# A 2-D Fourier layer whose residual rides through its own backward transform, with both w transforms as four 64x64 tiles

## The chip, the cores and the metric

One NeuronCore of one Trainium2 chip runs the whole program in one launch. The metric is device microseconds (us) of an execution; lower is better. A core has a tensor engine (PE, whose weight loads are listed apart as PEld), a vector engine (DVE), a scalar engine (ACT), GpSimd (POOL) and a sync engine (SP) that here issues all the transfers. Each engine runs its own instructions in order and waits on semaphores for the others.

## The reference, cut to what matters

`x` has two images of 48 x 48 tokens with 768 channels, float32.

```python
# --- layer 0: group norm, then attention over all 2304 tokens with relative positions
x = x + _L0_conv_ref(_gn(x), qkv_w, qkv_b, proj_w, proj_b, rel_pos_h, rel_pos_w)
# --- layer 1: group norm, then a block-diagonal complex MLP between two Fourier transforms
x = x + _L1_conv_ref(_gn(x), w1, b1, w2, b2)

def _L1_conv_ref(x, w1, b1, w2, b2):           # 8 blocks of 96 channels
    xf = jnp.fft.rfft2(x, axes=(1, 2), norm='ortho')          # 48 x 25 frequencies
    o1r = gelu(xr @ w1[0] - xi @ w1[1] + b1[0]);  o1i = gelu(xi @ w1[0] + xr @ w1[1] + b1[1])
    o2r = o1r @ w2[0] - o1i @ w2[1] + b2[0];      o2i = o1i @ w2[0] + o1r @ w2[1] + b2[1]
    xc = softshrink(o2r, 0.01) + 1j * softshrink(o2i, 0.01)
    return jnp.fft.irfft2(xc, s=(48, 48), axes=(1, 2), norm='ortho')
```

The second `x +` is the residual of this case: the layer's input has to be added to what the backward transform gives.

## The kernel before

All arithmetic is float32. Both images' attention comes first, in one pipelined loop (`attention`). Then, for each image in turn, come `project_out` and `Spectral.run`. Between the images, the second image's projection loads are prepared while the first image's spectral part ends.

`project_out` makes the output of layer 0 and starts the Fourier transform over w. There are 18 tiles of 128 tokens (t) in two halves of 384 channels (hf). `pr.product(t, hf)` is six matmuls into a PSUM bank called `acc`. `rows(i)` loads four 96-token rows of the input into a tile `x2[i]` (96 partitions hold two image rows) and POOL adds the projection bias, one instruction for each of the four. DVE adds the product onto `x2` (L941), in pieces given by `shifts(t)`, because 128-token tiles and 96-token rows do not line up. When two rows' worth is ready, `over_w(g)` multiplies it by the transform matrix `fw` (L920, banks `ps_y`), ACT copies the result to `y1` (L927), and SP writes it to a scratch tensor `y_d` in device memory. The first three products' six banks are already filled at the end of attention (`late.fill`).

`Spectral` works on four groups s of 192 channels, each of two blocks n of 96. `load` brings group s back from `y_d` (tiles `y2`, queue entries `y<-y_d`). `over_h(n)` is the transform over h (banks `ps_z`), `mean` and `norm` the group norm, `first(n)` and `second(n)` the two layers of the MLP (banks `ps_1`, `ps_2`). After the second block of a group, `back_h(j)` transforms back over h (banks `ps_u`) and writes a scratch tensor `u_d`. `back_w(s, more)` first, if s is at least 0, multiplies the loaded `u2` tiles by `iw` (L1213, banks `ps_x`). DVE adds the result onto `x2` (L1221), which has held the residual all along, and SP sends that part of `x2` to the output. In the same loop it loads the next group's `u2` from `u_d`. `back_w` is called with s = -1 at block 2, s = 0 at block 4, s = 1 at block 6, s = 2 at the end, and then s = 3 with `more=False`.

Seven PSUM banks are shared by everything except attention's `ps_o`. Order on an engine is chosen by the framework's scheduler from dependences; what goes through `InOrder` keeps its program order (and is recorded as L68, the helper's line, so such work is told apart by its tiles). SP's queue is in order too: an entry that waits holds up all entries behind it.

Of the kernel before, what the change touches and what calls it, by code (L numbers as in the profile page):

```python
# [42 lines left out]
YP = 112  # L43
# [232 lines left out]
def attention(tc, k, xs, a, oTs, inv_ds, late, span, ps_b, ps_o):  # L276
# [12 lines left out]
    with ExitStack() as ctx:  # L289
# [263 lines left out]
        def finish(un):  # L553

            pr, g, x = un["pr"], un["g"], un["x"]
            if x == 0:
                outs[pr, g] = outp.tile([P, 8, 3, 16], F32, tag="res", name="res")
                if g % 3 == 0:
                    dens[pr, g // 3] = outp.tile([P, 3, 2, 3], F32, tag="dens", name="dens")
            res = outs[pr, g]  # L560
            act.copy(res[:, :, x, :], un["o"][:, :P].rearrange("p (y d) -> p y d", d=16))
            dve.tensor_reduce(
                dens[pr, g // 3][:, x, :, g % 3], un["parts"], AX.X, ALU.add
            )
            if x == 2:
                sync.dma_start(
                    out=oTs[pr // NP][pr % NP * P : (pr % NP + 1) * P, g * UQ : (g + 1) * UQ],
                    in_=res.rearrange("p y x d -> p (y x d)"),
                )

        def inverses(pr, half):
# [12 lines left out]
            def send():  # L584
                dst = inv_ds[pr // NP][pr % NP, half].rearrange("h g (y x d) -> x (h g) y d", x=3, d=16)
                for x in range(3):
                    sync.dma_start(
                        out=dst[x],
                        in_=turned[6 * x : 6 * x + 6, :].rearrange("p (y d) -> p y d", d=16),
                    )  # L590
# [155 lines left out]
def shifts(t):  # L746


    size = {0: P, 32: 32, 64: 64, 96: 32}
    p = 0  # L750
    while p < P:
        hp, q = divmod(t * P + p, 2 * HW)
        n = min(P - p, 2 * HW - q, size[p], size[q])
        yield p, hp, q, n
        p += n


class Projection:
# [27 lines left out]
    def cut(self, whole, i):  # L786

        return whole[:, self.head + i * NCC * UQ :][:, : NCC * UQ]
# [10 lines left out]
    def w(self):  # L799
        return self.fixed()[:, : NCC * C].rearrange("p (cc f) -> p cc f", f=C)  # L800

    @property
    def pb(self):
        return self.fixed()[:, NCC * C : self.head]
# [82 lines left out]
def project_out(tc, k, x_b, pr, pools, y_d, x2, constants):  # L887
# [7 lines left out]
    ps_b, work = pools  # L895
    bank = lambda name: ps_b.tile([P, 512], F32, tag="b", name=name)
    R = 2 * HW
    x_v = x_b.rearrange("(t p) c -> p t c", p=R)

    def rows(i):  # L900

        part = x2[i]
        pr.sync.dma_start(out=part, in_=x_v[:, i * XP : (i + 1) * XP, :])
        for j in range(XP):
            pr.pool.tensor_tensor(part[:, j, :], part[:, j, :], pr.pb[:R], ALU.add)
# [4 lines left out]
    row = lambda hp: x2[hp // XP][:, hp % XP, :]  # L910

    def over_w(g, steps=range(C // SC)):

        y1 = work.tile([YP, 2, C], F32, tag="y1", name="y1")
        part = x2[2 * g // XP]
        t0 = 2 * g % XP
        for s in steps:
            ch = slice(s * SC, (s + 1) * SC)
            ps = bank("ps_y")
            nc.tensor.matmul(  # L920
                ps[:YP, : 2 * SC],
                lhsT=k.fw,
                rhs=part[:, t0 : t0 + 2, ch],
                start=True,
                stop=True,
            )
            nc.scalar.copy(y1[:, :, ch], ps[:YP, : 2 * SC].rearrange("p (t c) -> p t c", c=SC))  # L927
        ch = slice(steps[0] * SC, (steps[-1] + 1) * SC)
        pr.sync.dma_start(out=y_d[:, 2 * g : 2 * g + 2, ch], in_=y1[:, :, ch])

    turned = 0
    for t in range(NT):
        if t % 3 == 0 and 0 < t < NT - 3:
            pr.tokens(t // 3 + 1)
            rows(t // 3 + 1)
        for hf in range(2):
            cols = slice(hf * UQ, (hf + 1) * UQ)
            acc = pr.product(t, hf)
            for p, hp, q, n in shifts(t):
                dst = row(hp)[q : q + n, cols]  # L940
                nc.vector.tensor_tensor(dst, acc[p : p + n, :UQ], dst, ALU.add)  # L941
            if t == NT - 1:
                half = C // SC // 2
                for g in range(turned, HW // 4):
                    over_w(g, range(hf * half, (hf + 1) * half))
        while t < NT - 1 and (turned + 1) * 2 * R <= (t - 1) * P:
            over_w(turned)
            turned += 1
# [3 lines left out]
class Spectral:  # L952
# [12 lines left out]
    def __init__(self, tc, k, a, pools, x2, y_d, out_b, prepare):  # L965
        self.tc, self.nc, self.k, self.a, self.prepare = tc, tc.nc, k, a, prepare
        self.sync = InOrder(tc, tc.nc.sync)
        self.span, self.ps_b, self.small, self.wp, self.yp, self.up, self.dp, zp = pools
        self.x2, self.y_d = x2, y_d
        self.out_v = out_b.rearrange("(t p) c -> p t c", p=2 * HW)  # L970
# [21 lines left out]
        self.y2, self.u2, self.w, self.power = {}, {}, {}, {}  # L992
# [57 lines left out]
    def norm(self, n):  # L1050
# [24 lines left out]
        for f0 in range(0, NF, 400):  # L1075
            fs = slice(f0, f0 + 400)
            nc.gpsimd.tensor_tensor(self.both[n % 2][:, fs], zf[:, 0, fs], zf[:, 1, fs], ALU.add)

    def load(self, s, pieces):

        src = self.y_d[: 4 * KW, :, s * SC : (s + 1) * SC].rearrange(
# [7 lines left out]
    def over_h(self, n):  # L1089
# [7 lines left out]
        for j in range(KW // WP):  # L1097
# [13 lines left out]
            if n == 1 and j == 1:  # L1111
                self.mean(0)
            if n == 1 and j == 3:
# [30 lines left out]
    def second(self, n, ahead):  # L1144
# [9 lines left out]
        for j in range(KW // WP):  # L1154
# [22 lines left out]
            nc.gpsimd.tensor_tensor(val, val, clip, ALU.subtract)  # L1177
# [25 lines left out]

    def back_w(self, s, more):


        nc, k = self.nc, self.k
        ch = slice(s * SC, (s + 1) * SC)
        u_d = self.u_d.rearrange("w (q t) c -> (w q) t c", q=4)
        for i, part in enumerate(self.x2):  # L1210
            for t in range(0, XP, 2) if s >= 0 else ():
                ps = self.bank("ps_x")
                nc.tensor.matmul(  # L1213
                    ps[: 2 * HW, : 2 * SC],
                    lhsT=k.iw,
                    rhs=self.u2[s, i][:, t : t + 2, :],
                    start=True,
                    stop=True,
                )
                dst = part[:, t : t + 2, ch]  # L1220
                nc.vector.tensor_tensor(  # L1221
                    dst, ps[: 2 * HW, : 2 * SC].rearrange("p (t c) -> p t c", c=SC), dst, ALU.add
                )
            if more:
                u2 = self.up.tile([4 * KW, XP, SC], F32, tag="u2", name="u2")
                self.sync.dma_start(out=u2, in_=u_d[:, i * XP : (i + 1) * XP, :])
                self.u2[s + 1, i] = u2
            if s >= 0:
                self.sync.dma_start(
                    out=self.out_v[:, i * XP : (i + 1) * XP, ch], in_=part[:, :, ch]  # L1230
                )

    def run(self):
# [12 lines left out]
        for n in range(NBK + 1):  # L1246
# [6 lines left out]
            if n:  # L1253
                self.second(n - 1, ahead)
# [15 lines left out]
def block_kernel(tc, a, out):  # L1270
    nc = tc.nc
    B = a["x"].shape[0]
    with ExitStack() as ctx:
# [21 lines left out]
        for b in range(B):  # L1295
            oTs.append(dram.tile([C, S], F32, tag=f"oT{b}", name=f"oT{b}"))
            y_ds.append(dram.tile([YP, HW // 2, C], F32, tag=f"y_d{b}", name=f"y_d{b}"))
# [26 lines left out]
        attention(tc, k, a["x"], a, oTs, inv_ds, late, span, ps_b, ps_o)  # L1324
        for b in range(B):
            with ExitStack() as ctx2:
# [3 lines left out]
                x2 = [  # L1330
                    pool(f"x2_{i}", 1).tile([2 * HW, XP, C], F32, tag="x2", name=f"x2_{i}")
                    for i in range(HW // 2 // XP)
                ]
# [113 lines left out]
```

## Time and profile before

| what | value |
|---|---|
| median of 3 runs | 3661.01 us (3660.04 to 3662.53) |
| the profiled execution | 3660.19 us, span 3658.4 us |
| granted TensorE clock, mean | 0.987 |
| attention | to about 2838 us of the span |
| image 0: `project_out`, then `Spectral` | 2838 to 2988, then to about 3236 us |
| image 1: `project_out`, then `Spectral` | 3236 to 3409, then to 3658 us |

In the profile PE's and the other engines' busy times are of instructions that work, not of those that wait. A float32 matmul is recorded as two MATMUL rows. "idle before" is the time an engine sat idle just ahead of a group, and the arrow names what released it. Queue entries are listed under SPq with the time that their issue took.

### The profile page before, as it was taken

Reading aid. Unit: us, or ns where it says so; the run is one execution under the profiler, and the core shown is the slowest. Engines: PE = TensorE matmul, PEld = TensorE weight load, DVE = VectorE, ACT = ScalarE, POOL = GpSimd, SP = SyncE. Lnnn points to the kernel's source line nnn. Section 1 sums busy time; section 2 is a strip of 40 time slices with the busy share of each in tenths; the row PEclk is TensorE's granted clock in tenths of the full one; section 3 lists DMA queues with packets and bytes.
Section 4 is the critical chain, followed back from the end, with each engine's and each line's share of the span. In section 5 each row is a group of like instructions: output and inputs, shape, how many; then the busy total and the mean of one; then the engine's idle time right before and its main releaser. Section 6 shows DMA issues by size and latency. Waiting matters only on the chain.

```text
span 3658.4 us, 92606 instructions
## 1 busy us (share of the span) xinstructions
PE 3548.6 (97%) x36032; PEld 2477.2 (68%) x36032; DVE 2902.1 (79%) x6771; ACT 2557.2 (70%) x3769; POOL 2047.2 (56%) x662
## 2 busy tenths in 40 slices
PE   7999999999999999999999999999988999999898
PEld 5677676767767666677676767767666557655675
DVE  4798989989989996799898989899996437743576
ACT  3788888888888888688888888888885124301342
POOL 2567666757575763567666666666673524343232
PEclk9999999999999999999999999999999989999999
DMA  3687778777777885677777777777888743585434
GB/s 105 142 181 171 180 171 179 172 179 171 181 169 175 214 200 122 140 178 174 176 176 171 177 173 175 176 176 172 188 190 190 200 127 85 169 213 147 109 110 140
DMA packets 496484, 607.61 MB, mean 166 GB/s; under 512 B 179117, under 2 KB 311597, under 8 KB 496046
## 3 DMA queue, kind: packets, MB, share of 16 engines
q1 hardware_dynamic: 496046, 601.68, 69.3%
q8 instruction: 286, 4.69, 0.6%
q14 instruction: 152, 1.25, 0.1%
HBM read 131.60 MB, written 87.67 MB: 60 GB/s over the span
## 4 chain that ended last, share of the span: by engine, by line
PE 84%; DVE 5%; ACT 3%; DMA 3%; issue 2%; POOL 1%; SPq 1%; POOLq 0%; DVEq 0%; ACTq 0%
PE ps_o L68 22%; PE ps_s L68 21%; PE ps_proj L68 15%; PE ps_v L68 8%; PE acc L68 7%; DVE s L68 2%; PE ps_u L1195 2%; PE ps L1160 2%; PE ps_y L920 2%; PE ps_r L68 2%; SPq L68 1%; PE ps_x L1213 1%; DMA pT<-s 1%; ACT spectrum L1035 1%; POOL s L68 1%
## 5 line engine op out<-in xcount | busy, mean ns | idle before, releaser
L68 POOL TENSOR_TENSOR s<-rhw 128x2304 f32<-128x2304 f32 x432 | 1740.8, 4062 | 1025.3 <-DMA pT<-s 546.8
L68 DVE CUSTOM_DVE_ANT_0 s<-ps_s,s 128x512 f32<-128x512 f32 (+1 forms) x2160 | 1222.2, 633 | 299.7 <-issue 196.1
L68 ACT ACTIVATE s<-s,nm 128x1152 f32<-128x1152 f32 x864 | 1074.7, 1245 | 335.3 <-DVE nm L68 333.1
L68 DVE STREAM_TRANSPOSE s<-s 128x1152 f32<-128x1152 f32 x864 | 1112.0, 1344 | 6.8 <-ACT s L68 6.8
L68 ACT COPY pT<-s 32x1152 f32<-32x1152 f32 x864 | 993.6, 1150 | 25.9 <-PE ps_o L68 7.5
L68 PE MATMUL ps_o<-pT,v 128*64 128x128 f32 x15552 | 906.5, 276 | 41.7 <-ACT res L68 18.9
L68 PEld LDWEIGHTS ps_o<-pT,v 128*64 128x64 f32 x15552 | 875.4, 139 | 84.0 <-issue 43.6
L68 PE MATMUL ps_s<-kT,qT 64*128 64x512 f32 (+1 forms) x4320 | 899.8, 554 | 4.9 <-DVE mx L68 1.7
L68 PEld LDWEIGHTS ps_s<-kT,qT 64*128 64x128 f32 x4320 | 432.3, 186 | 418.1 <-issue 347.0
L68 PE MATMUL ps_proj<-xnT,w 128*64 128x384 f32 (+1 forms) x4032 | 591.3, 446 | 4.9 <-ACT xnT L68 3.7
L68 PEld LDWEIGHTS ps_proj<-xnT,w 128*64 128x64 f32 x4032 | 281.0, 137 | 278.8 <-issue 212.1
L941 DVE TENSOR_TENSOR x<-acc,x 32x384 f32<-32x384 f32 (+2 forms) x216 | 119.2, 553 | 227.8 <-PE acc L68 163.8
L68 PE MATMUL ps_v<-w,xnT 128*64 128x128 f32 x5184 | 297.3, 274 | 0.0
L68 PEld LDWEIGHTS ps_v<-w,xnT 128*64 128x64 f32 x5184 | 281.7, 137 | 21.2 <-DVE mx L68 21.2
L927 ACT COPY y<-ps_y 112x384 f32<-112x384 f32 x96 | 46.0, 479 | 299.5 <-PE ps_y L920 282.7
L68 DVE DVE_READ_ACCUMULATOR2_ANT mx<- 128x1 f32 x2160 | 179.7, 83 | 0.0
L68 ACT ACTIVATION_READ_ACCUMULATOR s<-s,nm 128x1 f32 x864 | 161.4, 187 | 0.0
L1177 POOL TENSOR_TENSOR spectrum<-spectrum 128x480 f32<-128x480 f32 x80 | 96.3, 1204 | 113.2 <-DVE spectrum L1176 85.0
L1160 PE MATMUL ps<-w,spectrum 96*64 96x96 f32 x3200 | 143.1, 248 | 0.0
L1160 PEld LDWEIGHTS ps<-w,spectrum 96*64 96x64 f32 x3200 | 133.6, 137 | 11.1 <-issue 4.4
L68 PE MATMUL acc<-proj_s 128*128 128x384 f32 x360 | 118.2, 486 | 0.4 <-POOL x L68 0.4
L68 PEld LDWEIGHTS acc<-proj_s 128*128 128x128 f32 x360 | 68.3, 190 | 48.2 <-POOL x L68 0.6
(139 smaller groups left out, 2299.8 us busy)
## 6 DMA issues: line engine op xcount, KB each, us to landing
pT<-s SPq DMA_DIRECT2D x2592, 144.0 KB
t<-rel SPq DMA_DIRECT2D x144, 189.0 KB
rhw<-t SPq DMA_DIRECT2D x144, 144.0 KB
y<-y_d SPq DMA_DIRECT2D x40, 360.0 KB
u_d<-spectrum SPq DMA_DIRECT2D x40, 360.0 KB
u<-u_d SPq DMA_DIRECT2D x48, 300.0 KB
w<-in_qkv_w SPq DMA_DIRECT2D x36, 384.0 KB
oT<-res SPq DMA_DIRECT2D x72, 192.0 KB
```

The source lines that it names most:

```text
L68: return lambda *args, **kw: self.tc.keep_in_program_order(op(*args, **kw))
L920: nc.tensor.matmul(ps[:YP, : 2 * SC], lhsT=k.fw, rhs=part[:, t0 : t0 + 2, ch], start=True, stop=True,)
L927: nc.scalar.copy(y1[:, :, ch], ps[:YP, : 2 * SC].rearrange("p (t c) -> p t c", c=SC))
L941: nc.vector.tensor_tensor(dst, acc[p : p + n, :UQ], dst, ALU.add)
L1035: self.nc.scalar.activation(junk, part, AF.Square, accum_out=total)
L1160: nc.tensor.matmul(ps[64 * r : 64 * r + 64, w * BS : (w + 1) * BS], lhsT=self.o1[:, ri, f0 : f0 + 64], rhs=w2[:, (0, 2, 1, 0)[2 * r + ri], ...
L1177: nc.gpsimd.tensor_tensor(val, val, clip, ALU.subtract)
L1195: nc.tensor.matmul(ps[: 2 * HW, :480], lhsT=k.ih, rhs=d2[:, c0 : c0 + 480], start=True, stop=True)
L1213: nc.tensor.matmul(ps[: 2 * HW, : 2 * SC], lhsT=k.iw, rhs=self.u2[s, i][:, t : t + 2, :], start=True, stop=True,)
```

## The change

- The residual no longer waits in SBUF. Each group's piece of the forward transform over w is fetched once more from `y_d` into tiles `yy` (laid out like `u2`). For groups 0 to 2 POOL adds `yy` to `u2` (in `second`, where `residual` holds: six additions in blocks 3, 5 and 7). For the last group PE does it, by transforming both terms into the same banks (`rows_of` with two terms). `x2` becomes short-lived tiles `x1`, three in rotation.
- Both w transforms use 64x64 tiles of PE. `over_w` and `back_w` put one image row at partitions 0 to 63 and the next at 64 to 127, and let two column halves of PE take two different moving operands: four matmuls of 384 columns where there were two. `x1` holds 128 partitions, 32 of them repeated (`rows` makes six transfers), and the projection's token order within a group of 384 is permuted (`res`, `turned` and `moves(t)` follow). A tile of `u2` or `yy` is filled by two transfers of 50 partitions; an output tile `ot` (three in rotation) is filled by one copy on DVE and one on ACT and sent in four transfers.
- At the end of `project_out` all products of the first 384 channels precede those of the second.
- `mean(0)` and `norm(0)` come one step earlier, POOL's work in `Spectral` is kept in program order, ten `y2` buffers replace eight, and the constants are loaded once. Twelve memsets of the `u2` and `yy` tiles are added ahead of image 0's `x1` additions on POOL.

```diff
 class Projection / finish / inverses: the permuted order of tokens
-            act.copy(res[:, :, x, :], un["o"][:, :P].rearrange("p (y d) -> p y d", d=16))
+            if x < 2:
+                act.copy(res[:, :, 0:3:2, 16 * x : 16 * x + 16], o)
+            else:
+                act.copy(res[:, :, 1, :].rearrange("p k (i d) -> p k i d", i=2), o)
...
 def project_out
-        part = x2[i]
-        pr.sync.dma_start(out=part, in_=x_v[:, i * XP : (i + 1) * XP, :])
+        part = rows_pool.tile([P, XP, C], F32, tag="x1", name="x1")
+        for q, i, w0, n in (
+            (0, 0, 0, 32), (32, 0, 32, 16), (48, 1, 32, 16),
+            (64, 1, 0, 32), (96, 0, 32, 16), (112, 1, 32, 16),
+        ):
+            pr.sync.dma_start(out=part[q : q + n], in_=x_v[g, i, w0 : w0 + n])
...
+    def over_w(n, halves=range(2)):
+        for hf in halves:
+            both = [bank(f"ps_y{i}") for i in range(2)]
+            for c in range(2):
+                for i in range(2):
+                    r = slice(64 * i, 64 * i + 64)
+                    pr.pe.matmul(
+                        both[i][64 * c : 64 * c + 64, :UQ],
+                        lhsT=k.fw[r, :],
+                        rhs=x1[g][r, k0 + c, cols],
...
+            for i in range(2):
+                nc.scalar.copy(y1[:, i, cols], both[i][:, :UQ])
+        for c in range(2):
+            pr.sync.dma_start(
+                out=y_v[2 * n + c, :, :, cols], in_=y1[64 * c : 64 * c + 2 * KW, :, cols]
             )
...
+        if t % 3 == 2:
+            over_w(2 * g)
+        elif t % 3 == 0 and g:
+            over_w(2 * g - 1)
+    for hf in range(2):
+        for t in range(NT - 3, NT):
+            outputs(t, hf)
+            if t == NT - 3:
+                if hf:
+                    over_w(c, (0,))
+                else:
+                    over_w(c - 2)
+        over_w(c - 1, (hf,))
+    over_w(c, (1,))
...
 def second
+            if residual and j > 1:
+                for part in (2 * j - 4, 2 * j - 3):
+                    self.pool.tensor_tensor(
+                        self.u2[part], self.u2[part], self.yy[part], ALU.add
+                    )
...
+    def fetch(self, tiles, src, j):
+        for i in range(2):
+            self.sync.dma_start(
+                out=tiles[j][64 * i : 64 * i + 2 * KW], in_=src[i][..., j * XP : (j + 1) * XP, :]
+            )
+    def rows_of(self, terms, both, first=True, last=True):
+        for x, term in enumerate(terms):
+            for m in range(2):
+                for i in range(2):
+                    r = slice(64 * i, 64 * i + 2 * KW)
+                    pe.matmul(both[i][64 * m : 64 * m + 64, : 2 * SC], lhsT=k.iw[r, :],
+                              rhs=term[r, 2 * m : 2 * m + 2, :], start=..., stop=...)
...
 def back_w
+        if more:
+            for j in range(HW // 2 // XP):
+                self.fetch(self.yy, y_v, j)
+        for j in range(3) if last else ():
+            ahead[j] = self.rows_of([self.yy[j]], banks(), last=False)
+        for j in range(HW // 2 // XP):
+            if s >= 0:
+                if j in ahead:
+                    both = self.rows_of([self.u2[j]], ahead[j], first=False)
+                elif last:
+                    both = self.rows_of([self.yy[j], self.u2[j]], banks())
+                else:
+                    both = self.rows_of([self.u2[j]], banks())
+                ot = self.op.tile([P, 2, 2, SC], F32, tag="ot", name="ot")
+                for i in range(2):
+                    self.copy(
+                        ot[:, i], both[i][:, : 2 * SC].rearrange("p (t c) -> p t c", c=SC)
+                    )
             if more:
+                self.fetch(self.u2, u_v, j)
             if s >= 0:
+                for m in range(2):
+                    for i in range(2):
+                        self.sync.dma_start(
+                            out=self.out_v[j, m, :, i, :, s * SC : (s + 1) * SC],
+                            in_=ot[64 * m : 64 * m + HW, i],
+                        )
```

The built program's queues show how SP's order moves. At the start of image 0's `project_out` the one load `x<-in_x` stood ahead of the last `oT<-res` and `inv_d<-turned`; now the first of six pieces stands there and five stand behind these. At the end of each image, 12 `yy` loads stand between the last `u_d` write and the `u2` loads, and 24 outputs of the last group ahead of image 1's last four pieces of `x1`. On PE, image 0's first `ps_y` matmuls now come right after attention's last work, ahead of the products of t = 3; image 1 has six products ahead of its first `ps_y` where it had eight.

## The prediction

> **What bounds the kernel now.** I read the page's engine shares and its chain of waits first, to see which engine an edit must touch.
>
> ```profile
> PE 3548.6 (97%) x36032; PEld 2477.2 (68%) x36032; DVE 2902.1 (79%) x6771; ACT 2557.2 (70%) x3769; POOL 2047.2 (56%) x662
> PE 84%; DVE 5%; ACT 3%; DMA 3%; issue 2%; POOL 1%; SPq 1%; POOLq 0%; DVEq 0%; ACTq 0%
> ```
>
> PE is busy nearly always and is 84% of the chain that ends last. So matmul time removed from a stretch where PE never waits is time gained, and a new PE wait there is time lost. The stages differ, so I asked for the groups by line over the stretch after attention.
>
> ```profile
> L1213 PE MATMUL ps_x<-u,iw 100*96 100x384 f32 x192 | 66.7, 499 | 7.9 <-DMA u<-u_d 6.6 <-DVE x L1221 1.3
> L920 PE MATMUL ps_y<-x,fw 96*112 96x384 f32 x184 | 64.0, 487 | 4.6 <-DVE x L941 4.6
> L68 POOL TENSOR_TENSOR x<-x,proj_s 96x768 f32<-96x768 f32 x20 | 35.5, 1810 | 12.7 <-DMA x<-in_x 12.7
> ```
>
> The two w transforms take 66.7 and 64.0 us of PE and hardly wait. These are what the tiles can shorten. Next, in the order of time, the places where transfers meet PE: SP's queue at the start of image 0's projection, then its end.
>
> ```profile
> 2818.30 0.56 SPq L68 DMA_DIRECT2D x<-in_x  x1
> 2837.84 0.34 SPq L68 DMA_DIRECT2D oT<-res  x1
> 2838.28 2.40 SPq L68 DMA_DIRECT2D inv_d<-turned  x3
> ...
> 2842.97 0.37 SPq L68 DMA_DIRECT2D x<-in_x  x1
> ```
>
> SP has issued the first load of the residual rows, then sits for 19 us until attention's last result is there. POOL's additions to those rows run from 2830.91 for 7.12 us, so the load was there in time. The next load, issued at 2842.97, let POOL start at 2850.76: 7.8 us from issue to use.
>
> ```profile
> 3630.55 4.12 SPq L1199 DMA_DIRECT2D u_d<-spectrum  x3
> 3637.37 0.29 SPq L68 DMA_DIRECT2D u<-u_d  x1
> ...
> 3644.44 10.05 SPq L68 DMA_DIRECT2D out<-x  x7
> ```
>
> At the end of an image PE has nothing but `ps_x`, paced by the loads of `u`. Last, the share of the 16 DMA engines in three stretches (the last two columns):
>
> ```profile
> 3068.00:3077.00 9.00, 9.00 (x137) 8.27 (x137) 5.11 (x10) 6.75 (x18) 3.14 (x4) 1.00 0.61 206
> 3642.00:3650.00 8.00, 5.47 (x16) 1.88 (x14) 4.24 (x8) 0.00 (x0) 0.00 (x0) 1.00 0.92 321
> 3652.00:3656.00 4.00, 1.50 (x4) 0.57 (x4) 1.36 (x3) 0.00 (x0) 0.00 (x0) 1.00 0.89 281
> ```
>
> The six `u` loads (100 partitions, 1.84 MB) stand alone in the first and use 0.61 of the engines, ten of 16, for 9 us. In the last 20 us of the span the engines are full. What is added there is added to the time.
>
> **The matmuls.** A chain of acc matmuls starts one 384-column row each 7.74 / 24 = 0.322 us. `over_w` has 96 such rows an image, 30.9 us. The change makes 192, each on a quarter of PE. The trace has no four at once, but both halves of it: `ps_s` (row halves, 64*128) needs 4.07 us for 20 rows that at 0.322 / 384 us a column would take 7.7, and `ps_v` (column halves, 128*64) 4.08 us for 72 rows that would take 7.7. So between two at once (30.9 us, no gain) and four (15.5 us). I take four, since rows and columns each double alone: -15.5 us an image, **-31.0**. The Trainium skill's page "TensorEngine Tiling (Array Packing)", Tiling Modes, speaks of four independent 64x64 tiles, for the upper end, and adds a rule against the change: going from one tiling to another drains the engine. No run here shows four.
>
> What a switch costs stands in the trace: `ps_o` to `ps_s` to `ps_v` costs 0.35 us above the pace (0.10 before the first `ps_s` pair and 0.10 after it, 0.15 at `ps_v`). The same full-array mode served `acc` and `ps_y` before; now each of 11 `over_w` is a switch in and out: 3.9 us an image, **+7.8**; bounds 0 and twice that.
>
> DVE's pieces go from 108 to 156 an image (13 for three tiles, for each of two halves, six times). At 0.553 us that is 26.5 us more beside 139 us of products, at most 5 x 0.553 = 2.8 us for each 3.87 us product, so covered, except where a bank or a `ps_y` waits for them. ACT's 48 copies stay 48.
>
> **Image 0's start.** Five of six pieces of the first `x1` now stand behind `oT<-res` (2837.84), then five `inv_d` issues where three took 2.40 us, so 4.0, then five issues of about 0.42: the last at 2844. With 4 to 7.8 us to landing (a first piece is there already) the rows are there at 2848 to 2852; I take 2850. POOL's twelve memsets (128 columns take 205 ns and 32 take 123, so about 0.75 each, 9 us) fit before that. Then POOL adds row by row (1.78 us each), DVE does 14 pieces in order, the first five paced by POOL, and the second half's `ps_y` can start about 10.5 us after the landing and is through at 2861.2. PE is in order and has nothing else: it stood at the same place at 2838.15 + 1.3 + 0.35 = 2839.8 without the delay. **+21.4**. Cover would be the products of t = 3, but they are queued behind. Bounds 12 (landing at 2841) and 24.
>
> **Between the images.** After the last `u_d` write (3216.1) come twelve `yy` loads: 1.84 MB, as much as the `u` loads, in 768-byte packets. Packets of that size take 36 to 46 ns, so 240 on each of ten engines 9.6 us, on all 16 6.0; I take ten, as the 100-partition `u` load shows. The Trainium skill's page "DMA: Bandwidth & Descriptors" ("How many engines") has the largest divisor up to 16 of the slowest dimension, ten for 50 partitions, and its rules for kernel authors advise against splitting a transfer in partition halves: both on the side of 9.6. `u2` and outputs follow for 15.0 us (before: 3219.96 to 3234.9), so PE gets to image 1's products at 3216.0 + 9.6 + 15.0 + 1.4 = 3242.0 instead of 3236.3: 5.7 later. The first `x1` is ready 5.7 later too, 3258.05 + 5.7 = 3263.8, and its `ps_y` through 11.2 later, 3275.0, when PE has been through its six products and could be there at 3242.0 + 23.2 + 1.65 = 3266.9: 8.1 more. **+13.8**, bounds 4 and 20. Before, eight products (31 us) hid this.
>
> **End of `project_out`.** First-half channels are written two products (7.7 us) before the end, not one; of the 3.0 us that `ps_z` waits for `y<-y_d` and the 2.3 us of waits on DVE I take 2 an image back (0 to 3), and from the earlier `norm(0)`, where `first(0)` waited 3.6, 1.5: **-7.0** for both images.
>
> **`back_w` in the middle** (s = 0, 1). PE saves 12 x 0.322 = 3.87 us each time with four tiles. But `ot` has three buffers, and its fourth copy waits until four outputs have landed, behind `yy` (9.6) and `u2` on the same engines: some 9 us after the first `ps_x`. Six of seven banks are held by then; the `ps_z` of `over_h` go one at a time through the seventh at about 1.9 us instead of 0.86, so its end comes where it came. I take **0**; bounds -3.5 and +3 each, -14 and +12. POOL's 18 additions an image (1.8 us, 33 us beside 85 of 233 busy) end before POOL's next block; a DVE operation that has to wait for one has slack.
>
> **Tail.** `yy` from 3635 to 3644.6 on ten engines; `u2` and outputs took 3637.4 to 3651.3, now to 3658.5; then 24 output issues where six were. At 0.32 + 0.06 us each they need 9.1 us of SP from about 3657: 3666.2, and 3.2 us to land, as the last output took, less what its quarter size saves (about 1.4): 3668, 1.2 more to the end, 3669.2. **+10.8**; bounds +4 and +14.
>
> Attention: two `inv_d` issues more for nine units, 0.75 us each, 24 times, on a queue that waits 472.5 us for DVE: 0, at most +3.
>
> Sum: -31.0 + 7.8 + 21.4 + 13.8 - 7.0 + 0 + 10.8 = +15.8. From the profiled 3660.2 (its span and 1.8 around it) that is 3676.0, and the median lies 0.8 above the profiled execution: **3677 us**.
>
> **Rivals.** (1) Only two tiles at once. Each `over_w` beyond the first costs 1.29 more (14.2 an image, and 0.6 at the first), `back_w` some 3 in all: 3677 + 29.6 + 3 = 3710. For it: no row has four. Against: both halvings are full. (2) Faster: the added transfers are absorbed. Place: the ten engines after each `u_d`. Price: `yy` hidden takes 5.7 from both the start of image 1 and its `x1` (the wait there falls by what PE then gains, to 8, so -5.7), `ot` comes free early (-14), and the tail is only SP's issues (+4, not 10.8): 3677 - 5.7 - 14 - 6.8 = 3650.5. It decides if `yy` delays `u2` by under some 3 us. For it: SP is idle just there for 2 us. Against: shares of 0.92 and 0.89. (3) The late `x1` costs 12, not 21.4, and the middle gains half its 14: 3661, no change.
>
> **How the numbers follow.** A measurement of this kernel tells about 0.2%, 7.3 us, from no change. Chances: forecast 0.52 (3664 to 3692), rival 1 0.14, rival 2 0.21, rival 3 0.13. Faster 0.21, same 0.14, slower 0.65. The range leaves out half of rival 1 and a part of rival 2: 3645 to 3708; the forecast's own is 3664 to 3692.
>
> **What would show it.** Four `ps_y` starts within some 30 ns and 0.65 us for eight rows: four tiles; starts in pairs and 1.29: rival 1. PE idle from 2838 to about 2857 with `x1` or DVE named: image 0's step. Acc of image 1 starting 5 us or more late after its last `u_d`: the between step. The last outputs ending some 33 us after the last `u_d` issue, not 23: the tail. `u2` landing no later than before would make the prediction wrong, as would `x1` loads ahead of attention's last results.

## The result: 129 us slower, 3.5%

| kernel | median of 4 runs | range | ratio to before, 95% interval |
|---|---|---|---|
| before | 3661.77 us | 3660.04 to 3664.65 | |
| changed | 3790.6 us | 3787.23 to 3796.93 | 1.0353 (1.0335 to 1.0371) |

The forecast was 3677 us, with 3708 as its upper end. The direction was right, the size was not. Of the profiled executions, the spans are 3658.4 and 3785.6 us: 127.2 us to account for.

The page of the changed kernel, its engine shares and its chain that ended last:

```profile
PE 3572.7 (94%) x36512; PEld 2476.8 (65%) x36512; DVE 2941.3 (78%) x6819; ACT 2572.5 (68%) x3817; POOL 2116.8 (56%) x710
PE 81%; DMA 5%; DVE 5%; issue 2%; ACT 2%; SPq 2%; POOL 2%; DVEq 0%; ACTq 0%; POOLq 0%
```

DMA has risen from 3% to 5% of the chain. PE's share of the span falls from 97% to 94%, and yet it is busy 24 us longer, although it has less to do. Both are to be explained: PE waits more, and it works more slowly. The mean granted clock is 0.963, after 0.987.

Where the time went, stage by stage, from the starts of the tiles' groups on PE in the two traces. "Group s" is the first `ps_x` of `back_w` with that s. The forecast's terms are put into the same stages.

| stage | image | before us | changed us | difference | forecast |
|---|---|---|---|---|---|
| to the end of attention on PE | | 2837.7 | 2841.1 | +3.4 | 0 |
| to the first `ps_z` | 0 | 150.6 | 164.4 | +13.8 | +7.8 |
| first `ps_z` to group 0 | 0 | 129.4 | 137.8 | +8.4 | -1.5 |
| group 0 to group 2 | 0 | 96.3 | 124.9 | +28.6 | 0 |
| group 2 to image 1's `acc` | 0 | 22.2 | 42.1 | +19.9 | +5.7 |
| `acc` to the first `ps_z` | 1 | 173.6 | 173.2 | -0.4 | -5.5 |
| first `ps_z` to group 0 | 1 | 126.7 | 134.0 | +7.3 | -1.5 |
| group 0 to group 2 | 1 | 96.3 | 119.3 | +23.0 | 0 |
| group 2 to the end | 1 | 25.5 | 48.6 | +23.1 | +10.8 |

The largest term, 51.6 us between the groups' `ps_x`, was forecast at 0.

**The middle.** PE groups of the changed kernel after attention (line, engine, tiles, busy us and mean ns of one, idle before and what ended it):

```profile
L1142 PE MATMUL ps_z<-fh,y 96*96 96x96 f32 x800 | 95.8, 289 | 30.2 <-DVE spectrum L1183 14.1 <-DMA y<-y_d 9.9 <-DVE spectrum L1042 3.0
L1242 PE MATMUL ps_u<-spectrum,ih 128*96 128x480 f32 x160 | 76.5, 613 | 24.1 <-POOL spectrum L67 24.1
L67 PE MATMUL ps_y<-x,fw 64*64 64x384 f32 x384 | 52.0, 514 | 22.1 <-DVE x L965 22.1
L67 PE MATMUL ps_x<-yy__29569,iw 50*64 50x384 f32 x16 | 4.8, 776 | 27.3 <-ACT ot L1044 22.8 <-DMA yy__29569<-y_d 4.5
```

The same two groups in the kernel before:

```profile
L1100 PE MATMUL ps_z<-fh,y 96*96 96x96 f32 x800 | 80.1, 264 | 7.6 <-DMA y<-y_d 7.4
L1195 PE MATMUL ps_u<-spectrum,ih 128*96 128x480 f32 x160 | 70.2, 578 | 7.7 <-POOL spectrum L1177 7.7
```

`ps_z` waited 7.6 us there and `ps_u` 7.7. Now they wait 30.2 and 24.1, most of it for DVE (and `y2` loads) and for POOL, and are themselves longer (95.8 after 80.1, 76.5 after 70.2). PE's timeline behind the first `ps_x`, before and then changed, shows the first cause:

```profile
3117.74 7.91 PE L1213 MATMUL ps_x<-u,iw 100*96 100x384 f32 x24
3125.48 4.41 PE L1100 MATMUL ps_z<-fh,y 96*96 96x96 f32 x50
3129.83 1.87 PE L1160 MATMUL ps<-w,spectrum 96*64 96x96 f32 x40
...
3131.89 5.17 PE L1160 MATMUL ps<-w,spectrum 96*64 96x96 f32 x120
```

```profile
3146.64 0.82 PE L67 MATMUL ps_x<-u__29568,iw 50*64 50x384 f32 x8
3147.39 1.09 PE L1142 MATMUL ps_z<-fh,y 96*96 96x96 f32 x10
3149.23 1.09 PE L1142 MATMUL ps_z<-fh,y 96*96 96x96 f32 x10 [0.75 <-DVE spectrum L1042]
...
3156.86 3.47 PE L1202 MATMUL ps<-w,spectrum 96*64 96x96 f32 x40
...
3160.67 8.23 PE L1202 MATMUL ps<-w,spectrum 96*64 96x96 f32 x120
```

`ps_z` goes ten rows at a time through the one bank that is left, since `ps_x` holds the others until `ot` is free. It takes 9.5 us instead of 4.4. Then the same `ps` groups that took 1.87 and 5.17 us before take 3.47 and 8.23. The windows of these two stretches (length, then busy time of PE, PEld, DVE, ACT and POOL, then the granted clock, the DMA share and GB/s) say why:

```profile
3147.39:3156.93 9.54, 6.65 (x56) 5.74 (x54) 1.31 (x2) 4.17 (x11) 0.00 (x0) 0.81 0.57 173
3156.93:3168.90 11.97, 11.97 (x163) 11.61 (x163) 5.70 (x12) 1.81 (x6) 2.43 (x3) 0.58 0.49 150
```

PE was busy 6.65 of 9.54 us, never idle for more than 0.75 us at once, and the granted clock fell while this went on: 0.81 over the stretch, then 0.58 over the next 12 us, in which PE had no wait at all. The Trainium skill's page "TensorE: Matmul & The Clock Gate" (A second HAM failure mode: psum-queue depth-cycling) tells of another kernel in which such short idles between banks throttle PE. This trace agrees, with 0.58.

The second cause is in POOL and DVE, at block 5 of image 0. DVE's timeline:

```profile
3178.36 6.02 DVE L1115 TENSOR_SCALAR w<-w,nm_rstd 96x288 f32<-96x288 f32 x1
3184.31 0.55 DVE L1183 TENSOR_TENSOR spectrum<-spectrum,ps_1r 96x400 f32<-96x400 f32 x1
```

The scaling of `w` takes 0.41 us when it is alone, as in the kernel before. Here it lasts 6.02 us, while POOL goes from one instruction to the next (`both`, `spectrum`, an addition of `yy`, from 3178.26 to 3184.17), and 7.78 in the second image, where a further addition is through before it ends. What PE needs is queued behind it on DVE, as PE's timeline shows:

```profile
3184.91 5.12 PE L1142 MATMUL ps_z<-fh,y 96*96 96x96 f32 x30 [6.03 <-DVE spectrum L1183]
```

The Trainium skill's page "SBUF — State Buffer" (SBUF: two separate sides) has a port pair that DVE and POOL lock for a whole instruction. The trace fits this, and here DVE is held over several of POOL's instructions in a row; the lock itself is not in the records.

The third is on POOL at block 7, first POOL's timeline, then PE's:

```profile
3247.04 1.80 POOL L67 TENSOR_TENSOR u__29567<-u__29567,yy__29573 128x768 f32<-128x768 f32 x1 [1.74 <-DMA u__29567<-u_d]
3250.32 1.80 POOL L67 TENSOR_TENSOR u__29568<-u__29568,yy__29574 128x768 f32<-128x768 f32 x1 [1.48 <-DMA u__29568<-u_d]
3252.08 3.51 POOL L67 TENSOR_TENSOR spectrum<-spectrum 128x480 f32<-128x480 f32 x3
```

```profile
3253.33 3.52 PE L1242 MATMUL ps_u<-spectrum,ih 128*96 128x480 f32 x4 [7.27 <-POOL spectrum L67]
```

The additions wait for the last `u2` loads. POOL keeps its program order, so the `spectrum` work that `ps_u` waits for stands behind them: 7.27 us of PE, and `ps_u` then takes 3.52 instead of 1.85, at half clock.

**The ends.** SP's queue after image 0's last `u_d`:

```profile
3271.46 1.32 SPq L67 DMA_DIRECT2D yy__29569<-y_d  x2
...
3278.58 1.72 SPq L67 DMA_DIRECT2D u__29563<-u_d  x2
3280.35 2.83 SPq L67 DMA_DIRECT2D out<-ot  x4
3283.76 1.52 SPq L67 DMA_DIRECT2D u__29564<-u_d  x2
...
3300.06 1.52 SPq L67 DMA_DIRECT2D u__29568<-u_d  x2
```

`yy` takes 7.1 us of issues; then each round of two loads and four outputs takes about 4.3 us. The last `u2` pair is issued 29 us after the last `u_d`. The DMA engines are not full meanwhile: 0.61, 0.56 and 0.49 in three windows of 8 us from 3280, where the kernel before had 0.86 from 3216 to 3236. A `u2` load costs SP 0.71 us (median), where `u` cost 0.43, and there are twice as many. The loads also arrive more slowly: in the packet records, the 3072-byte packets of `u2` are 4.1 at a time on average from 3280 to 3304 (never over 8) and under way for 20.4 of these 24 us, where those of `u` were 9.7 at a time in the stretch of the kernel before in which they stand alone (3068 to 3077).

On PE, `ot` holds the banks here too, since its outputs stand behind `yy` in the queue:

```profile
3275.47 0.83 PE L67 MATMUL ps_x<-yy__29569,iw 50*64 50x384 f32 x2 [2.85 <-DMA yy__29569<-y_d]
3287.98 0.91 PE L67 MATMUL ps_x<-yy__29569,iw 50*64 50x384 f32 x3 [11.69 <-ACT ot L1044]
...
3310.41 2.29 PE L67 MATMUL acc<-proj 128*128 128x384 f32 x3
```

**Image 0's start**, SP's timeline and PE's:

```profile
2841.22 0.35 SPq L67 DMA_DIRECT2D oT<-res  x1
2841.61 3.83 SPq L67 DMA_DIRECT2D inv_d<-turned  x5
2845.48 2.32 SPq L67 DMA_DIRECT2D x<-in_x  x5
```

```profile
2840.81 0.28 PE L67 MATMUL ps_i<-ident,inv 128*18 128x128 f32 x1
2858.82 1.51 PE L67 MATMUL ps_y<-x,fw 64*64 64x384 f32 x2 [17.73 <-DVE x L965]
...
2862.94 4.81 PE L67 MATMUL ps_y<-x,fw 64*64 64x384 f32 x12 [0.86 <-DVE x L965]
```

PE waits 17.73 us, and then DVE's pieces stretch the first `ps_y` to 8.9 us, where an undisturbed one takes 1.52.

### The profile page after: what moved, and what is told of

It reads as the page before. It is cut to its first block, busy times and chain, and to the rows that moved or that the text cites. A ratio compares the mean times of both kernels' runs of the same rounds, so it can differ in the third digit from the quotient of the medians.

```text
span 3785.6 us, 94710 instructions
## 1 busy us (share of the span) xinstructions
PE 3572.7 (94%) x36512; PEld 2476.8 (65%) x36512; DVE 2941.3 (78%) x6819; ACT 2572.5 (68%) x3817; POOL 2116.8 (56%) x710
## 4 chain that ended last, share of the span: by engine, by line
PE 81%; DMA 5%; DVE 5%; issue 2%; ACT 2%; SPq 2%; POOL 2%; DVEq 0%; ACTq 0%; POOLq 0%
PE ps_o L67 21%; PE ps_s L67 20%; PE ps_proj L67 14%; PE ps_v L67 8%; PE acc L67 7%; PE ps L1202 3%; SPq L67 2%; DVE s L67 2%; PE ps_z L1142 2%; PE ps_r L67 1%; DMA pT<-s 1%; PE ps_u L1242 1%; ACT pT L67 1%; PE ps_y L67 1%; PE ps_x L67 1%
## 5 line engine op out<-in xcount | busy, mean ns | idle before, releaser
L965 DVE TENSOR_TENSOR x<-acc,x 32x384 f32<-32x384 f32 (+2 forms) x312 | 173.0, 554 | 180.4 <-PE acc L67 91.3
L952 ACT COPY y<-ps_y 128x384 f32<-128x384 f32 x96 | 40.3, 490 | 288.4 <-issue 148.1
L1202 PE MATMUL ps<-w,spectrum 96*64 96x96 f32 x3200 | 159.0, 262 | 5.3 <-DVE spectrum L1212 5.3
L1202 PEld LDWEIGHTS ps<-w,spectrum 96*64 96x64 f32 x3200 | 147.9, 147 | 20.2 <-issue 10.9
L1142 PE MATMUL ps_z<-fh,y 96*96 96x96 f32 x800 | 95.8, 289 | 30.2 <-DVE spectrum L1183 14.1
L67 PE MATMUL acc<-proj_s 128*128 128x384 f32 x360 | 119.3, 489 | 0.0
```

The lines of the kernel that those rows point to most:

```text
L67: return lambda *args, **kw: self.tc.keep_in_program_order(op(*args, **kw))
L952: nc.scalar.copy(y1[:, i, cols], both[i][:, :UQ])
L1142: nc.tensor.matmul(ps[:BS, w * 96 : (w + 1) * 96], lhsT=self.y2[s, j][:, w, i * BS : (i + 1) * BS], rhs=k.fh, start=True, stop=True,)
L1202: nc.tensor.matmul(ps[64 * r : 64 * r + 64, w * BS : (w + 1) * BS], lhsT=self.o1[:, ri, f0 : f0 + 64], rhs=w2[:, (0, 2, 1, 0)[2 * r + ri], ...
```

## The experiments

Theory A: the matmuls gain what was forecast, and the loss is the residual's new way: POOL's additions, `ot` in three buffers that holds banks until the clock falls, and SP's longer queue at the ends. Theory B: PE in 64x64 tiles is granted a lower clock afterwards. The table has the stages that decide, image 0 / image 1, in us. They are from one profiled execution of each kernel, whose time lies up to 10 us from the median (e8: 3759.17).

| kernel | median | ratio (95% interval) | group 0 to 1 | group 1 to 2 | group 2 to `acc` / to the end of the last `ps_x` |
|---|---|---|---|---|---|
| before | | | 56.7 / 56.7 | 39.6 / 39.6 | 22.2 / 20.6 |
| changed | 3790.6 | 1.0353 | 74.9 / 72.8 | 50.0 / 46.5 | 42.1 / 39.9 |
| e1 | 3724.86 | 1.0168 (1.0153 to 1.0183) | 59.7 / 58.8 | 40.3 / 40.0 | 33.9 / 33.5 |
| e2 | 3748.59 | 1.0229 (1.0207 to 1.0251) | 63.1 / 62.7 | 46.0 / 38.9 | 41.9 / 40.7 |
| e3 | 3767.26 | 1.0281 (1.0264 to 1.0298) | 57.6 / 57.6 | 50.6 / 46.7 | 38.3 / 37.2 |
| e8 | 3768.74 | 1.0282 (1.0266 to 1.0298) | 64.5 / 65.7 | 39.8 / 38.9 | 42.0 / 39.8 |
| e9 | 3737.43 | 1.0198 (1.0183 to 1.0213) | 54.0 / 54.0 | 36.0 / 35.9 | 47.0 / 39.4 |
| e4 | 3706.22 | 1.0114 (1.0095 to 1.0132) | 54.1 / 54.1 | 36.1 / 36.1 | 31.1 / 30.9 |
| e5 | 3688.53 | 1.0070 (1.0055 to 1.0085) | 54.1 / 54.1 | 36.1 / 36.1 | 32.1 / 29.7 |
| e6 | 3685.81 | 1.0064 (1.0049 to 1.0079) | 54.1 / 54.1 | 36.1 / 36.1 | 20.6 / 18.1 |
| e7 | 3678.73 | 1.0037 (1.0025 to 1.0048) | 54.1 / 54.1 | 36.1 / 36.1 | 20.7 / 18.8 |
| e10 | 3661.84 | 0.9995 (0.9986 to 1.0004) | 54.5 / 54.1 | 36.1 / 36.1 | 19.6 / 18.5 |
| e11 | 3654.0 | 0.9976 (0.9964 to 0.9987) | 54.5 / 54.1 | 36.1 / 36.1 | 19.5 / 16.8 |

**e1: the residual left out.**

```diff
-            for j in range(HW // 2 // XP):
-                self.fetch(self.yy, y_v, j)
-        for j in range(3) if last else ():
-            ahead[j] = self.rows_of([self.yy[j]], banks(), last=False)
...
-                    both = self.rows_of([self.yy[j], self.u2[j]], banks())
+                    both = self.rows_of([self.u2[j]], banks())
...
-            if residual and j > 1:            # POOL: u2 += yy, with the lines under it
```

> The changed kernel without its residual: no yy loads, no additions on POOL, no second term on PE in the last group (the residual is left out of the result). The 64x64 tiles, ot in three buffers and the split transfers stay. Theory A (the loss is the residual's new way: additions on POOL that wait for loads and hold DVE, yy in front of u2 in SP's queue): the gaps of PE ahead of ps_u and ps_z in the middle (6.0, 7.3, 7.7 and 5.7 us in the changed kernel) go, 7.3 us of SP issues go at each image's end, together with the clock lost behind them about 50 us: 3740. Theory B (PE in 64x64 tiles is granted a lower clock afterwards): the stretches at clock 0.50 behind ps_x stay, only the two ends gain some 15 us: 3775.

66 us less than the changed kernel, rather more than theory A said. Some waits of up to 3.0 us stay behind `ps_x`, where copies into `ot` still wait for their buffers, and the clock is still 0.50 for a while behind the first of them (3150 to 3154), but most of the middle's loss is gone. That is against theory B, since the tiles are all still there.

**e2: POOL's additions alone left out**, and **e3: six buffers for `ot`.**

```diff
-            if residual and j > 1:            # e2, with the lines under it
...
-                rest = lambda: (pool("sp_o", 3), pool("sp_w", 2), pool("sp_z", 1))     # e3
+                rest = lambda: (pool("sp_o", 6), pool("sp_w", 2), pool("sp_z", 1))
```

> The changed kernel without the eighteen additions of yy to u2 on POOL in each image (the residual of groups 0 to 2 is left out); yy is still loaded, and the last group still adds it on PE. Theory A: the four gaps of 6 to 8 us ahead of ps_u and ps_z go, and the 0.50 clock after them: 30 us less, 3760. If the additions are harmless and the loads are what costs (rival C): under 8 us less, over 3780.

> The changed kernel with ot in six buffers in place of three. Theory A: copies out of ps_x no longer wait for outputs to land, banks come free, ps_z of the block behind ps_x takes 4.4 us and not 9.5, and the clock behind it stays at 1.00: about 10 us at s = 0 and 4 at s = 1 in each image, 28 in all, some more at the ends: 3755. Theory B: ps_z gets its banks but the clock still falls to 0.50 some 8 us behind ps_x: 10 us less at most, 3780.

42 and 23 us less (forecast 30 and 35). In e3, PE's timeline behind the same `ps_x`:

```profile
3149.42 0.82 PE L67 MATMUL ps_x<-u__29568,iw 50*64 50x384 f32 x8
3150.17 4.49 PE L1142 MATMUL ps_z<-fh,y 96*96 96x96 f32 x50
3154.59 1.87 PE L1202 MATMUL ps<-w,spectrum 96*64 96x96 f32 x40
...
3156.65 5.17 PE L1202 MATMUL ps<-w,spectrum 96*64 96x96 f32 x120
```

All fifty rows run through, and the `ps` groups behind them take their old 1.87 and 5.17 us. The granted clock is 1.00 there. This settles theory B: the tiles don't lower the clock, the waits for banks do.

e3 does more than free the banks, though. POOL's additions of block 5 now meet DVE's scaling of `w` at another moment. It lasts 1.93 us, and PE's wait of 6.03 us for DVE is 0.18 us. What e3 leaves is POOL's order at block 7. Both in its PE timeline:

```profile
3171.97 2.79 PE L1142 MATMUL ps_z<-fh,y 96*96 96x96 f32 x30 [0.18 <-DVE spectrum L1183]
...
3240.04 3.52 PE L1242 MATMUL ps_u<-spectrum,ih 128*96 128x480 f32 x4 [12.41 <-POOL spectrum L67]
```

PE gets there sooner, the additions still wait for `u2`, and the 7.27 us have become 12.41. So from group 1 to group 2 e3 gains nothing (50.6 and 46.7 us, after 50.0 and 46.5), and its total falls short of the forecast.

**e8: POOL's order left to the scheduler.**

```diff
-self.sync, self.pool = InOrder(tc, tc.nc.sync), InOrder(tc, tc.nc.gpsimd)
+self.sync, self.pool = InOrder(tc, tc.nc.sync), tc.nc.gpsimd
```

> The changed kernel, with POOL's work in Spectral no longer kept in program order (the scheduler places the additions of yy to u2). If the additions cost because those that wait for u2 hold up POOL's later work (theory A): the scheduler can put them behind the work that PE waits for, and the gaps of 7 us ahead of ps_u go: 10 to 25 us less, 3770. If they cost by holding DVE (both read and write SBUF at once): within 6 us of the changed kernel.

22 us less, 3769 for 3770. All additions are done, and from group 0 to group 2 it is as good as e2, which has none: 208.9 us in the four stretches, beside 210.7 in e2 and 244.2 in the changed kernel. So it is their place in POOL's queue that costs there, more than their number. DVE's scaling of `w` at block 5 is back to 0.42 us (0.41 in e2).

**e9: e2 and e3 together.**

> The changed kernel without POOL's additions of yy to u2 (groups 0 to 2 are left without their residual) and with six ot buffers: the two separate causes of the loss between the ps_x of one group and the next taken away together. Theory A: nothing is lost there any more, 54 and 36 us from ps_x to ps_x as with the residual in SBUF, and the savings of e2 and e3 add: some 65 us less than the changed kernel, 3725. The start of image 0 and the two ends keep their loss. If a third cause sits there: ps_x to ps_x stays above 58 and 41 us, over 3740.

The middle is 54.0 and 36.0 us: nothing is lost any more. Over the four stretches e2 and e3 save 33.5 and 31.7 us alone and 64.3 together, but that these numbers add is chance. From group 0 to group 1 the savings overlap, since either edit alone also ends most of the wait at block 5: 54.4 us when summed over both images, 39.7 together. From group 1 to group 2 each edit alone leaves the other's wait in place: 10.8 us summed, 24.6 together. So neither saving is the price of one cause.

The total was 12 us above the expected one. In image 0 group 2 starts earlier, but its `ps_x` then waits 6.55 us for ACT. Its end takes 47.0 us instead of 42.1, yet from the last `u_d` issue to `acc` it is 35.6, after 39.3. In image 1 PE waits 7.52 us for the first rows of `x1`, whose loads stand behind 24 outputs, and the projection is 7 us longer than in the changed kernel.

**e4: the residual kept in SBUF, as before, under the new tiles.** The six `x1` tiles stay, DVE adds `ps_x` onto them, and the rows and columns of `ih` and `iw` are ordered so that a result lands where its residual is.

```diff
+                    dst = self.x1[j][:, 2 * i : 2 * i + 2, ch]
+                    nc.vector.tensor_tensor(dst, both[i][:, : 2 * SC]..., dst, ALU.add)
...
+                for q, i, w0, n in ((0, 0, 0, HW), (64, 1, 0, 32), (112, 1, 32, 16)):
+                    self.sync.dma_start(out=self.out_v[j, i, w0 : w0 + n, :, ch], in_=self.x1[j][q : q + n, :, ch])
```

> The changed kernel with the old kernel's residual: the twelve pieces of x1 of both images stay in SBUF in the new layout (six tiles, used again by the second image), DVE adds ps_x onto them and they are the output, in three transfers for each tile; no yy, no ot, no additions on POOL; eight y2 buffers. Rows of u are ordered so that a result lands on the half that holds its residual. The 64x64 tiles of both transforms, the late x1 of the first image and the rest of the change stay. Theory A: the middle of Spectral is as before and gains 3.8 us at each ps_x, so 15 in all, project_out gains 4 in the second image, the first image still loses some 17 at its start, the ends some 5 each: 3665 (3650 to 3685). Theory B: it loses some 16 us an image behind ps_x: over 3690.

3706 us, 84 less than the changed kernel and outside my 3650 to 3685. The middle is 2.6 and 3.5 us shorter than in the kernel before, so there the tiles' gain arrives. The start (164.2 us to `ps_z`) is as late as in the changed kernel, and the ends are still 9 and 10 us too long, twice what I had put for them. The next three runs are about that.

**e5: image 0's first rows by ACT's queue; e6: plain loads of `u2` and joined outputs; e7: both**, all on e4.

```diff
+            (nc.scalar if g == 0 and k.early else pr.sync).dma_start(...)      # e5
...
-u_v = self.u_d.rearrange("w (i r t) c -> i w r t c", i=2, r=2)                 # e6
+u_v = self.u_d.rearrange("w (r i t) c -> i (w r) t c", i=2, r=2)
-            if s >= 0:
+            if s % 2 == 1 and s > 0:     # outputs of groups s - 1 and s together
```

> The kernel with the residual kept in SBUF, and in image 0 alone the six loads of the first x1 tile are issued by ACT ahead of attention's last copies, so that they don't stand behind oT and inv_d in SP's queue. If the late x1 is what keeps PE idle after attention (17.5 us, and 6.5 more of ps_y paced by DVE): PE starts ps_y within some 3 us of attention's end and it is 15 to 22 us less than with the loads on SP. If POOL's additions or DVE's fourteen pieces bound the start (rival): under 8 us less.

> The kernel with the residual kept in SBUF, with two changes to its transfers: u_d's rows are ordered (r i t), so that a u2 load is 50 plain partitions of one stretch, and outputs are sent for two groups at once (after s = 1 and after s = 3), so eighteen output issues stand behind the last u2 loads and none between them. If the issues on SP set the ends (six times 2 x 0.75 and 3 x 0.45 us, 20 us): u2 issues fall to about 0.4 us, the stretch from the last ps_x of s = 2 to the next image's acc falls from 31 to about 20 us, the end by some 5: 15 to 20 us less than e4. If the transfers themselves set it (rival): the u2 loads take 9 us for 1.84 MB anyway and the joined outputs are late at the end: 0 to 5 us less.

> Both of the edits, first rows of x1 by ACT's queue and the plain and joined transfers, on the kernel with the residual kept in SBUF. If the two are as they should be and add up: some 35 us less than with neither, 3670, about the kernel before. If start and ends have a second cause: over 3690.

e5: 17.7 us less. In the profiles 10.0 us of the difference lie in the stretch to image 0's first `ps_z` (164.2 to 154.2), 4.1 in an earlier end of attention, which the edit does not explain. e6: 20.4 less. SP's timeline of e6 at image 0's end:

```profile
3231.76 0.31 SPq L1238 DMA_DIRECT2D u_d<-spectrum  x1
...
3235.06 0.67 SPq L67 DMA_DIRECT2D u__29587<-u_d  x2
...
3245.11 23.43 SPq L67 DMA_DIRECT2D out<-x  x18
3268.57 5.78 SPq L67 DMA_DIRECT2D x<-in_x  x9
```

A load now costs 0.31 us (median) instead of 0.72, the last is issued 9 us after the last `u_d`, and the stretch to `acc` is 20.6 us, below the 22.2 of the kernel before. So the layout and the order of these transfers set the end. Which part of it counts is not shown: with the issues, the loads themselves have become faster (the 3072-byte packets are 9.4 at a time from 3235 to 3244, where e4 has 4.2 from 3242 to 3262), and the outputs no longer stand between them. The next image's first rows now stand behind eighteen outputs, at 3268.57. e7 saves 27.5 us of the 35 expected: PE waits 8.73 us for these rows ahead of image 1's first `ps_y`, where e4 has 3.32.

**e10: `over_w` one product later; e11: and image 1's first rows issued after half of the outputs.**

```diff
-        if t % 3 == 2:                        # e10
-            over_w(2 * g)
-        elif t % 3 == 0 and g:
-            over_w(2 * g - 1)
+        if t == NT - 4:
+            over_w(2 * g)
+        elif t % 3 < 2 and g:
+            over_w(2 * g - 2 + t % 3)
...
+            if not more and j == 2 and k.ahead is not None:      # e11, in back_w
+                load_rows(self.sync, k.ahead, self.x1[0], 0)
```

> e7 with project_out's over_w one product later (over_w(0) after the products of t = 3, not t = 2, as the kernel before had it). If ps_y(0) being paced by DVE's pieces costs PE the 9.6 us it takes (1.5 when it doesn't wait), twice: PE does the products of t = 3 meanwhile, and 6 us are gained in each image: 3667. If x1 is what everything waits for, only shifted: under 4 us.

> e10, and the second image's first x1 loads are issued after the third tile's outputs of the last group, and not after all eighteen output issues. If x1 behind the outputs is the 8.7 us that PE waits ahead of ps_y in image 1: some 9 us less than e10, 3658, about or just below the kernel before. If the transfers share the engines anyway and outputs are then late (rival): 0 to 3 us less.

16.9 and 7.8 us less (forecast 12 and 9): 3661.8, then 3654.0. PE's timeline at image 0's start in e7, then in e11:

```profile
2845.26 0.28 PE L67 MATMUL ps_i<-ident,inv 128*18 128x128 f32 x1
2850.42 1.51 PE L67 MATMUL ps_y<-x,fw 64*64 64x384 f32 x2 [4.89 <-issue]
2852.14 1.54 PE L67 MATMUL ps_y<-x,fw 64*64 64x384 f32 x2 [0.21 <-DVE x L966]
2854.54 5.49 PE L67 MATMUL ps_y<-x,fw 64*64 64x384 f32 x12 [0.86 <-DVE x L966]
```

```profile
2842.20 0.28 PE L67 MATMUL ps_i<-ident,inv 128*18 128x128 f32 x1
2844.47 8.26 PE L67 MATMUL acc<-proj_s 128*128 128x384 f32 x24 [1.99 <-POOL proj_s L67]
2852.66 1.38 PE L67 MATMUL ps_y<-x,fw 64*64 64x384 f32 x8
2856.12 0.88 PE L67 MATMUL ps_y<-x,fw 64*64 64x384 f32 x8 [2.08 <-DVE x L971]
```

With early rows alone, PE still goes at DVE's pace: 9.6 us for what takes 1.5. With a product between, it works meanwhile. e10 can't be told from the kernel before, and e11 is faster than it by 0.24% (0.13 to 0.36%): it keeps the 64x64 tiles of the change and gives up the residual's way through the transform.

## Why the prediction was wrong, point by point

**The tiles: right.** The `ps_x` matmuls of one group, now 48 records where there were 24, take 4.10 us where they took 7.90 (forecast: 3.87 less). From one `over_w` over two products to the next is 17.13 us (2903.03 to 2920.16), after 18.06: 0.93 us gained, where the sum had 1.29 - 0.35 = 0.94. So four do run at once, rival 1 is out, and both switches together cost 0.36 us, as forecast. The Trainium skill's page "TensorEngine Tiling (Array Packing)" (Tiling Modes) says that a change of tiling drains the engine. The 0.36 us agree with it; the drain itself is not in the records.

**The middle: the step that failed.** "I take 0; bounds -3.5 and +3 each" stands against 51.6 us in all, the largest part of the 127. Three of its sentences were wrong. "So its end comes where it came" saw rightly that `ps_z` goes through one bank, but set the 5 us against the tiles' gain and left out the clock, which was 0.50 for some 12 us and doubled PE's time there (5 us more). That the additions "end before POOL's next block" counted POOL's busy time, but not that each addition waits for its `u2` load and holds up what stands behind it. "A DVE operation that has to wait for one has slack" had only one addition in mind; the scaling of `w` waited for a whole chain, and PE 6.03 us with it. e9, without the additions and with six `ot` buffers, has nothing of the loss left. How much belongs to each of the three can't be read from e2 and e3 alone, since they act on one another.

**The ends: mechanism half right, size wrong.** `yy` first does delay `u2`: its issues take 7.1 us, and its packets are about 11 at a time, near the ten assumed. But "`u2` and outputs follow for 15.0 us" was carried over from before, and with the 1.4 us to `acc` it took 31.8 for 16.4 (from the first `u2` issue at 3278.58 to `acc` at 3310.41). This is the mis-sized term: a `u2` load costs SP 0.71 us where `u` cost 0.43, there are twice as many, their packets are 4 at a time and not ten, four output issues stand between two pairs, and `ot` holds the banks. e4 and e6 show it in place: 42.1 us, 31.1 without `yy` and `ot`, 20.6 with the plain loads ahead of the outputs. At the tail it is +23.1 for +10.8, of which 19.3 up to the last `ps_x`. The second half of the step between the images came about as said: image 1's first `ps_y` lasts 7.9 us (3336.54 to 3344.44), 6.4 more than an undisturbed one, where 8.1 were forecast.

**Image 0's start: right.** 17.73 us of waiting and 7.4 of a stretched `ps_y`, 25 for the forecast 21.4: the rows were used at 2856.34, not 2850. SP's issues ended 3.8 us later than forecast, and 3.4 of that is attention's own later end.

**End of `project_out` and `norm(0)`: wrong in sign**, -3.5 an image forecast (1.5 of it in this stage), and +8.4 and +7.3 measured from the first `ps_z` to group 0. Of that, 5.3 and 3.1 lie behind the first matmul of `first(0)`; e2, without the additions of block 3, has 1.7 and 1.0 there. The rest, up to that matmul (+3.1 and +4.2), stayed in most of the later kernels and was not taken apart. In image 0 `ps_z` waits 5.9 us for `y2` loads, after 3.0. In image 1 it waits no longer than before (4.0 us, after 4.3), but the granted clock is 0.52 over the first 25 us, after 0.73.

**Attention: just over the edge**, +3.4 for 0 to 3. In the other kernels, whose attention is the same, it ends 3 to 8 us later than before. This stays open.

**Rivals.** Rival 2, that the added transfers are absorbed, hung on `yy` delaying `u2` by under some 3 us. The first `u2` issue comes 7.5 us behind the last `u_d` write in image 0, where it came 3.9 behind, so this is out. The gain of the middle in rival 3 needed it to be free of new waits. It would have been, with six `ot` buffers and without POOL's additions. That the direction came true says little for the sum: its largest term stood at 0.

## What to carry to other kernels

When an engine that paces everything is held up in small pieces, price the clock too: 5 us of lost bank turns became 10. An addition that waits for a load is not a cost of its own length but of everything queued behind it, so look at the queue and not at the share of busy time. When two edits that remove two causes save as much together as apart, compare them stage by stage before calling the causes separate. And for a transfer that is split or reordered, read both the issue time of its own shape and how many of its packets are under way at once; here both became worse together, and one edit mended both.

## What the runs showed of the hardware that was not expected

- PE's granted clock fell to 0.50 in a stretch in which PE was busy 70% of 9.5 us with no idle time over 0.75 us. In 2 us windows it is 1.00 from 3150 to 3152, 0.85 in the next and 0.50 from 3154.
- One DVE instruction of 0.41 us lasted 6.02 and 7.78 us beside a chain of POOL instructions, and so was held over several of them in a row. In e3, beside a chain like it, it lasted 1.93.
- A load of 50 partitions whose source is 25 x 2 rows took SP 0.71 us to issue, and its packets were 4 at a time; the same bytes from 50 plain rows took 0.31, and the packets were 9 at a time. It is not the number of strides alone: a `yy` load, 50 rows of four pieces, took 0.42 (medians).
- Row and column halves, seen only apart before, do combine: 48 matmul records of 64x64 tiles of 384 columns in 4.10 us.
